# The sync engine's transfers in program order, with the dependent ones placed later

## The chip, the cores and the metric

The kernel runs on one core of a Trainium2 chip. Its time is the device time of one execution in microseconds (us). Five engines work at once: TensorE (PE in the profile; its weight loads are PEld), VectorE (DVE), ScalarE (ACT), GpSimd (POOL) and SyncE (SP). SP computes nothing; it issues all of this kernel's DMA transfers, one after the other, and when the transfer at its head has to wait for data or for a buffer, everything behind it waits too.

## The reference

The input x has 8 sequences of 1024 tokens with 256 values each. The computation is an attention layer and a linear layer, each between a normalization in front and one behind, and each added to its input:

```python
x = x + layernorm(attention(layernorm(x), Wq, Wk, Wv, Wo))
x = x + layernorm(ternary_linear(layernorm(x), weight, alpha, bias))

def attention(x):                       # 16 query heads of 16 values, 4 key/value heads
    q, k, v = x @ Wq, x @ Wk, x @ Wv
    q, k = rope(q), rope(k)             # pairs of values rotated by the token's position
    scores = q k^T / sqrt(256)          # every query with all 1024 keys of its sequence
    return (softmax(scores) @ v) @ Wo

def ternary_linear(x):                  # weights become -1, 0 or 1
    d = 0.7 * mean(|weight|)
    return x @ ((weight > d) - (weight < -d)).T * alpha + bias
```

## The kernel before

**Blocks, groups, windows.** The work is cut into 16 blocks of 512 query tokens (units u = 0 to 15, two for each sequence). A block has four groups; a group i is one query head of each of the four key heads (in the last block, one tile of 128 tokens) against all 1024 keys. The inner loop (`window`, line 1137) runs over s, which counts the exp tiles: 32 a group, 128 a block, 2048 in all. One window takes two or three of them, about 2 us. In a window TensorE multiplies queries and keys for the exp tiles (`exp_one`, line 684; tile se, line 676), ScalarE takes the exponential (line 692, tile e), and TensorE multiplies e of two windows earlier with the values (`av_piece`, line 704, tile av).

**The maxima.** The softmax needs the largest score of each query. The scores are therefore computed twice. Some 40 exp tiles ahead, TensorE computes them in another layout (`max_scores`, line 586; tile sm, line 603) and DVE reduces them (line 628, tile mx). When a group is reduced, its maxima are transposed on TensorE and copied by ScalarE (`shift_rows`, line 649), and DVE makes the second part of them (`shift_low`, line 656, tile ml, line 660). Two DMA transfers on SP then write ml into four rows of the query tile `q_st` (line 667). The exp product of the group multiplies those rows with -1, so the maximum is subtracted inside the product. The first exp product of a group cannot start before its ml has landed.

**Queries and keys.** `q_st` has two buffers, one for each of two successive blocks; `k_st` holds the keys of a sequence and has three. They are made by `Project` two to three blocks ahead. `kv_and_dram` (line 428) multiplies keys and values, stores the keys to DRAM (d_k, line 434) and fetches them back in another layout (k_rot, line 438). `kt` (line 440) rotates and splits them on GpSimd, stores them (dk, line 451) and calls `stack_keys` (line 495), which loads them into `k_st` by six transfers (line 502). `q` rotates and splits the queries on GpSimd and `q_to_dram` (line 487) stores them (dq, line 493). At the start of block u-1 `stack_queries(u)` (line 562) loads them into `q_st`: six transfers of 256 KB (line 567) and two small fills (line 146).

**The tail.** The sums of a group leave through ScalarE (`av_out`, line 720, tile avsb) to DRAM (d_av, line 733). In the block after, `Tail` finishes the layer: it loads x again (xr, line 743), fetches the heads (`fetch`, line 759: two xn and den, lines 763 and 768), inverts the sums on DVE (`invert`, line 772), stores them and loads them back spread out (d_rec line 775, a line 780), scales and splits on GpSimd (`scale`, line 785), multiplies with Wo (`attn`), normalizes, runs the second layer (`xw`, `ffn`), normalizes again (`stats_f`) and stores the output (`end`, line 856).

**The order.** Lists of (step, part) say at which step of four exp tiles each part of a projection (`P_PARTS`) or a tail (`T_PARTS`, and `T_LAST` for the last but one) is issued. At the end of a window `collect` takes the parts that are due into `ready`, and `do_parts` issues them in order; parts that need a PSUM bank (`banked`) come one at a time, in windows of two exp tiles. A part can therefore be issued some windows after its step. For TensorE, DVE and ScalarE this order of issue is the order on the engine: the loop stands in `manual_schedule` for these three. The order on SP and on GpSimd is chosen at build time by a planner that goes by estimated times.

Of the kernel before, what the change touches and what calls it, by code (L numbers as in the profile page):

```python
# [8 lines left out]
F32 = mybir.dt.float32  # L9
# [7 lines left out]
P = 128  # L17
# [11 lines left out]
def kernel(  # L29
# [29 lines left out]
    nc = tc.nc  # L59
    B, S, D = x.shape  # L60
    DK = HKV * HD
# [15 lines left out]
    qkp = ctx.enter_context(tc.tile_pool(name="qkp", bufs=1))  # L77
# [29 lines left out]
    for src, lo, n in ((w_q, 0, D), (w_k, D, DK), (w_v, ROT, DK)):  # L107
        nc.sync.dma_start(
            out=wqkv[:, :, lo : lo + n], in_=src.rearrange("(c p) n -> p c n", p=P)
# [18 lines left out]
    nc.sync.dma_start(out=bias_bc, in_=bias.partition_broadcast(P))  # L128
    alpha_bc = const.tile([P, 1], F32, name="alpha_bc")
    nc.sync.dma_start(out=alpha_bc, in_=alpha.partition_broadcast(P))  # L130


    k_st, v_aug, q_st = [], [], []
# [30 lines left out]
    def split(eng, hi, lo, src, hi_eng=None):  # L164

        split_hi(hi_eng or eng, hi, src)
        split_lo(eng, lo, src, hi)
# [25 lines left out]
    ffn = {}  # L193
# [52 lines left out]
    def ln_apply(eng, dst, src, stats):  # L246
        mv, sc = stats
        for t in range(src.shape[1]):
            if eng is nc.scalar:
                eng.activation(dst[:, t, :], src[:, t, :], AF.Identity, bias=sc[:, 0, t : t + 1])  # L250
                eng.mul(dst[:, t, :], dst[:, t, :], sc[:, 1, t : t + 1])
                continue
            eng.tensor_scalar(  # L253
                dst[:, t, :],
                src[:, t, :],
                sc[:, 0, t : t + 1] if eng is nc.gpsimd else mv[:, t, 0:1],
                sc[:, 1, t : t + 1],
                ALU.add if eng is nc.gpsimd else ALU.subtract,
                ALU.mult,
            )  # L260
# [52 lines left out]
    def rotate(eng, x, cos, sin, t2):  # L313

        for dst, table in ((t2, sin), (x, cos)):
            eng.tensor_tensor(dst, x, table.unsqueeze(1).to_broadcast(list(x.shape)), ALU.mult)  # L316
        eng.tensor_tensor(x[:, 0], x[:, 0], t2[:, 1], ALU.subtract)
        eng.tensor_tensor(x[:, 1], x[:, 1], t2[:, 0], ALU.add)
# [5 lines left out]
    class Project:  # L324
# [103 lines left out]
        def kv_and_dram(self):  # L428

            u = self.u  # L430
            for p in range(2):
                self.kv(p)
            d_k = dram.tile([DK, UQ], F32, tag="d_k", name=f"d_k_{u}")
            nc.sync.dma_start(out=d_k, in_=self.kv_t[:DK])
            self.k_rot = qkp.tile([P, 2, P], F32, tag="k_rot", name=f"k_rot_{u}")
            src = d_k.rearrange("(m e) (g t) -> e g m t", e=2, t=P)
            for e in range(2):
                nc.sync.dma_start(out=self.k_rot[:, e, :], in_=src[e])

        def kt(self):  # L440
            rotate(
                self.eng, self.k_rot, cos_kt_sb[:, self.half], sin_kt_sb[:, self.half],
                work.tile([P, 2, P], F32, tag="t2k", name=f"t2k_{self.u}", bufs=1),
            )
            hl = qkp.tile([P, 2, 2, P], F32R, tag="k_parts", name=f"ks_{self.u}")
            split(self.eng, hl[:, 0], hl[:, 1], self.k_rot)
            dk = self.dk = dram.tile([2, DK, UQ], F32, tag="dk", name=f"dk_{self.u}")
            dst = dk.rearrange("l (m e) (g t) -> l e g m t", e=2, t=P)
            for l in range(2):
                for e in range(2):  # L450
                    nc.sync.dma_start(out=dst[l, e], in_=hl[:, l, e, :].bitcast(F32))
            self.stack_keys()

        def q_product(self, p):
            if self.q_rot is None:
# [31 lines left out]
        def q_to_dram(self):  # L487
            dq[self.u] = dram.tile([2, D, UQ], F32, tag="dq", name=f"dq_{self.u}")
            rows = dq[self.u].rearrange("l (b c i e) t -> l c b i (e t)", c=2, e=2, i=HD // 2)
            for l in range(2):  # L490
                for c in range(2):
                    src = self.hl["q"][64 * c : 64 * (c + 1), l].rearrange("p e t -> p (e t)")
                    nc.sync.dma_start(out=rows[l, c], in_=src.bitcast(F32))
# [242 lines left out]
    class Tail:  # L736
# [21 lines left out]

        def fetch(self):

            for c in range(2):
                self.on[c] = self.new("xn", c)
                nc.sync.dma_start(
                    out=self.on[c].rearrange("p t d -> p (t d)"),
                    in_=d_av[self.u][8 * c : 8 * c + 8, 0:HD, :],
                )
            self.den = small.tile([P, UQ // 8], F32, tag="den", name=f"den_{self.u}", bufs=1)
            nc.sync.dma_start(
                out=self.den, in_=d_av[self.u][:, HD, :].rearrange("i (g t) -> i g t", g=8)
            )  # L770

        def invert(self):
            nc.vector.reciprocal(self.den, self.den)
            d_rec = dram.tile([2, 2 * HKV, UQ], F32, tag="d_rec", name=f"d_rec_{self.u}")
            nc.sync.dma_start(
                out=d_rec.rearrange("c i (g t) -> (c i g) t", g=8), in_=self.den
            )
            for c in range(2):
                self.a[c] = self.new("a", c)
                nc.sync.dma_start(  # L780
                    out=self.a[c].rearrange("p t d -> p (t d)"),
                    in_=d_rec[c].unsqueeze(1).to_broadcast([2 * HKV, HD, UQ]),
                )
# [66 lines left out]
        def end(self, p):  # L850
            u, f = self.u, self.a[p]
            ln_apply(self.eng(p), f, f, self.sc[p])
            self.eng(p).tensor_tensor(f, self.x1[p], f, ALU.add)
            b, half = divmod(u, UPB)
            tiles = out[b, half * UQ : (half + 1) * UQ, :].rearrange("(t p) d -> p t d", p=P)
            nc.sync.dma_start(out=tiles[:, self.tiles(p), :], in_=f)

    class LastTail(Tail):

# [101 lines left out]
    def load(u):  # L961
# [12 lines left out]
        (29, "attn", 2), (29, "x", 1), (30, "stats_a", 2), (30, "ffn", 1), (31, "stats_f", 1),  # L974
    )
    T_PARTS = (
        (1, "fetch"), (7, "invert"), (8, "scale", 0), (9, "scale", 1), (12, "attn", 0),
        (15, "attn", 1), (15, "stats_a", 0), (17, "stats_a", 1), (19, "stats_x", 0),
        (22, "xw", 0), (23, "stats_x", 1), (26, "ffn", 0), (27, "xw", 1), (31, "ffn", 1),
        (31, "stats_f", 0), (33, "stats_f", 1),  # L980
    )

    P_FIRST = (47, 51, 54, 57, 59, 60, 62, 61, 63, 64)
    T_LAST = (1, 3, 4, 5, 9, 10, 11, 14, 17, 19, 20, 22, 25, 27, 24, 28)

    warm = []

# [64 lines left out]
    for u in range(NU - 1):  # L1052
        start = SPU * (u + 1)
        at(start + 1, begin_tail, u)
        steps = [k for k, *_ in T_PARTS] if u < NU - 2 else T_LAST
        for k, (_, *p) in zip(steps, T_PARTS):
# [15 lines left out]
    REGULAR = 40  # L1072
# [5 lines left out]
    def window_size(s):  # L1078


        left = 4 * NK - s % (4 * NK)
        if s >= ends:
            return 4
        if s == 6:
            return 2
        size = min(2 if s >= REGULAR and any(banked(*p) for p in ready) else 3, left, ends - s)
        if left - size == 1:
            size += 1 if size == 2 else -1
        return size
# [23 lines left out]
    def take_low():  # L1113
        while split_later:
            shift_low(split_later.pop(0))
# [12 lines left out]
    def av_windows(lag):  # L1128

        while len(behind) > lag:  # L1130
            i, s, size = behind.pop(0)
            first = s % (4 * NK)
            av_piece(i, first * P, (first + size) * P)
            if first + size == 4 * NK:
                done.append(i)

    def window(s):


        late, size = s >= ends, window_size(s)  # L1140
        if done:
            av_out(done.pop())
        if late:
            for r2 in range(2):
                exp_two(s // 4, r2)
        else:
            end = min(maxima_by(s + size), 4 * NSTEP)
            for q in range(max(size, end - maxima[0])):
                if q < size:
                    exp_one(s + q)  # L1150
                if maxima[0] < end:
                    max_scores(maxima[0])
                    maxima[0] += 1
                if q == 0:
                    take_low()
            reduce_early(maxima[0])
        take_low()
        behind.append((s // (4 * NK), s, size))
        for n in range(s // 4, (s + size) // 4):
            collect(n)  # L1160
        do_parts(3 - size if REGULAR <= s < ends else 99)
        av_windows(1 if late else 2)
        return s + size

    E = mybir.EngineType
    due, picks = [], []
    with tc.manual_schedule(engines={E.PE, E.DVE, E.Activation, E.Pool}):
# [52 lines left out]
        s = 0  # L1220
        while s < 8:
            s = window(s)
    with tc.manual_schedule(engines={E.PE, E.DVE, E.Activation}):
        while s < 4 * NSTEP:
            s = window(s)
        av_windows(0)
        av_out(NU * G - 1)
        assert not (todo or due or ready or split_later)
# [70 lines left out]
```

## Time and profile before

| what | value |
|---|---|
| median of 3 runs | 1698.6 us (1697.74 to 1701.16) |
| the profiled execution, its own time | 1696.64 us |
| its span from the first to the last instruction | 1694.9 us |
| TensorE busy | 1598.8 us, 94% of the span |
| DVE busy | 1398.7 us, 83% |
| ScalarE busy | 1246.4 us, 74% |
| GpSimd busy | 838.5 us, 49% |
| mean granted clock of TensorE | 0.972 |
| DMA moved | 117.95 MB, mean 70 GB/s, nearly all by SP's queue |

The profile is one execution on the chip. In its lines an instruction is named by its line of the kernel and by the tiles it writes and reads (out<-in). A line of a group ends with the busy time, the mean duration of one in ns, the idle time of its engine just before such instructions, and what ended most of it. A wait line reads: who waited, for whom, us in total, how many times, the longest. The chain of waits follows the work that ended last back through what released each step; its lines hold the start, the duration and what it was, and a DMA there runs from its issue to its landing. A timeline line of SP holds the time of issue and how long SP took to issue. The granted clock is the share of full speed that TensorE was given. In a line of a window (from:to) there are the length, the busy time and count of each engine, the granted clock, the share of time that the 16 DMA engines were busy, and GB/s; that share is the sum of the packets' times and can be a little over 1.

### The profile page before, as it was taken

The numbers are of one execution on the slowest core, as the hardware profiler recorded it, in microseconds if no ns is written. First come the engines' busy times: TensorE is split into PE (matmuls) and PEld (weight loads), VectorE is DVE, ScalarE is ACT, GpSimd is POOL, SyncE is SP. The second block draws the span as 40 slices with busy tenths as digits, with TensorE's granted clock in tenths as the row PEclk, the third lists the DMA queues.
The fourth block names the chain that finished last, engine by engine and source line by source line (L and its number), as shares of the span: only waits on it lengthen the run. The fifth ranks groups of instructions, "written<-read, shape, count | busy, mean of one in ns | idle before, by whom it ended". The sixth has DMA issues, their size and how long they took to land.

```text
span 1694.9 us, 36717 instructions
## 1 busy us (share of the span) xinstructions
PE 1598.8 (94%) x14440; PEld 811.3 (48%) x14440; DVE 1398.7 (83%) x2054; ACT 1246.4 (74%) x2423; POOL 838.5 (49%) x1239
## 2 busy tenths in 40 slices
PE   7989899999999999999999999999999999999997
PEld 5544454444545444444444445444444544444444
DVE  7778788979798797978889798797978879998864
ACT  4657677778687786877778687686867768787875
POOL 5541456374554646455464645536455453333444
PEclk8999999999999999999999999999999999999999
DMA  4151514125151432515133151412415124141100
GB/s 134 51 98 37 122 43 95 54 73 98 48 98 57 81 72 65 113 42 100 49 86 80 54 115 45 94 55 71 88 46 100 36 76 74 33 85 33 41 14 26
DMA packets 86077, 117.95 MB, mean 70 GB/s; under 512 B 12088, under 2 KB 50808, under 8 KB 85752
## 3 DMA queue, kind: packets, MB, share of 16 engines
q1 hardware_dynamic: 85904, 115.60, 29.4%
q8 instruction: 114, 1.87, 0.5%
q14 instruction: 59, 0.48, 0.1%
HBM read 68.65 MB, written 45.88 MB: 68 GB/s over the span
## 4 chain that ended last, share of the span: by engine, by line
PE 59%; DVE 22%; DMA 9%; POOL 3%; issue 3%; SPq 2%; ACT 2%; POOLq 0%; ACTq 0%; DVEq 0%
PE av L712 21%; PE se L676 19%; DVE mx L628 18%; PE sm L603 8%; PE pa L302 3%; DMA q_st<-ml 2%; PE pq L302 2%; PE pf L302 2%; DMA dk<-ks 2%; DMA k_rot<-d_k 2%; PE pkv L302 1%; DVE bnst L237 1%; PE pt_ot L279 1%; DMA d_k<-kv_t 1%; ACT e L692 1%
## 5 line engine op out<-in xcount | busy, mean ns | idle before, releaser
L628 DVE TENSOR_REDUCE mx<-sm 128x2 f32<-128x1024 f32 (+1 forms) x1309 | 1205.2, 970 | 244.5 <-PE sm L603 191.3
L692 ACT ACTIVATE e<-se 128x512 f32<-128x512 f32 x1996 | 1053.2, 603 | 301.4 <-PE sm L603 256.6
L603 PE MATMUL sm<-k_st,q_st 64*128 64x512 f32 x2048 | 756.6, 453 | 16.6 <-DVE mx L628 7.7
L676 PE MATMUL se<-q_st,k_st 64*128 64x512 f32 x2048 | 721.7, 448 | 48.4 <-DMA q_st<-ml 42.7
L712 PE MATMUL av<-e,v_aug 128*32 128x256 f32 (+2 forms) x8560 | 612.1, 383 | 0.0
L676 PEld LDWEIGHTS se<-q_st,k_st 64*128 64x128 f32 x2048 | 330.0, 187 | 418.6 <-ACT e L692 240.2
L603 PEld LDWEIGHTS sm<-k_st,q_st 64*128 64x128 f32 x2048 | 329.1, 188 | 94.5 <-DVE mx L628 73.3
L712 PEld LDWEIGHTS av<-e,v_aug 128*32 128x32 f32 x8560 | 196.7, 109 | 233.6 <-issue 171.6
L241 POOL TENSOR_SCALAR lnsc<-mv 128x2 f32<-128x2 f32 (+1 forms) x134 | 25.8, 193 | 287.2 <-DVE mv L239 280.8
L786 POOL TENSOR_TENSOR xn<-xn,a 128x512 f32<-128x512 f32 x30 | 38.5, 1284 | 156.3 <-DMA a<-d_rec 153.9
L242 POOL TENSOR_TENSOR lnsc<-lnsc,mhalf 128x2 f32<-128x2 f32 (+1 forms) x134 | 92.5, 691 | 0.9
L846 POOL TENSOR_TENSOR a<-a,bias_bc 128x512 f32<-128x512 f32 x30 | 38.6, 1285 | 97.9 <-ACT a L845 97.9
L253 POOL TENSOR_SCALAR xn<-x,lnsc 128x256 f32<-128x256 f32 x116 | 65.1, 569 | 2.2
L157 POOL TENSOR_SCALAR ot<-ot 128x512 fp32r<-128x512 f32 x30 | 18.6, 621 | 83.9 <-ACT ot L283 63.7
L316 POOL TENSOR_TENSOR t<-q_rot,sin_q_sb 128x512 f32<-128x512 f32 x31 | 39.8, 1285 | 39.9 <-ACT q_rot L460 39.9
L157 POOL TENSOR_SCALAR xt<-xt 128x512 fp32r<-128x512 f32 x26 | 16.2, 622 | 65.3 <-ACT xt L283 65.3
L302 PE MATMUL pq<-xt,wqkvh 128*128 128x256 f32 x256 | 47.9, 313 | 0.4 <-ACT e L692 0.4
L302 PE MATMUL pa<-woh,hl 128*128 128x256 f32 x240 | 46.2, 294 | 1.1 <-ACT e L692 1.1
L237 DVE BATCH_NORM_STATS2 bnst<-x 128x6 f32<-128x256 f32 x124 | 45.9, 412 | 0.6 <-DMA x<-in_L_attn_x 0.6
L237 DVE BATCH_NORM_STATS2 bnst<-a 128x6 f32<-128x256 f32 x120 | 44.5, 413 | 0.0
L302 PEld LDWEIGHTS pq<-xt,wqkvh 128*128 128x128 f32 x256 | 38.3, 208 | 13.0 <-issue 11.6
L162 POOL TENSOR_TENSOR hlq<-q_rot,hlq 128x512 fp32r<-128x512 f32 x31 | 39.5, 1275 | 7.0 <-ACT hlq L159 4.5
(165 smaller groups left out, 1298.0 us busy)
## 6 DMA issues: line engine op xcount, KB each, us to landing
q_st<-dq SPq DMA_DIRECT2D x90, 256.0 KB
dq<-hlq SPq DMA_DIRECT2D x60, 256.0 KB
d_av<-avsb SPq DMA_DIRECT2D x60, 256.0 KB
x<-in_L_attn_x SPq DMA_DIRECT2D x15, 512.0 KB
xn<-d_av SPq DMA_DIRECT2D x30, 256.0 KB
a<-d_rec SPq DMA_DIRECT2D x30, 256.0 KB
xr<-in_L_attn_x SPq DMA_DIRECT2D x15, 512.0 KB
out_x<-a SPq DMA_DIRECT2D x30, 256.0 KB
```

The costliest lines, as they stand in the source:

```text
L162: eng.tensor_tensor(lo, src, hi.bitcast(F32), ALU.subtract)
L237: nc.vector.bn_stats(st[:, t, :], src[:, t, :])
L242: nc.gpsimd.tensor_tensor(sc[:, 1, :], sc[:, 1, :], mhalf[:, :n], ALU.pow)
L253: eng.tensor_scalar(dst[:, t, :], src[:, t, :], sc[:, 0, t : t + 1] if eng is nc.gpsimd else mv[:, t, 0:1], sc[:, 1, t : t + 1], ALU.add i ...
L302: nc.tensor.matmul(out, chunk(left[i], c), chunk(right[j], c), start=(k == 0), stop=(k == len(steps) - 1),)
L316: eng.tensor_tensor(dst, x, table.unsqueeze(1).to_broadcast(list(x.shape)), ALU.mult)
L603: scores = nc.tensor.matmul(sm[0][:, part, :], queries[rows], k_st[(u // UPB) % 3][rows, r2, ch * 512 : (ch + 1) * 512], start=True, stop= ...
L628: early[0] = nc.vector.tensor_reduce(mx[i][:, a, head_and_tile(i, r2, t), lo:n], sm[0][:, lo:n, :], AX.X, ALU.max).ins
L676: nc.tensor.matmul(sc if len(queries.shape) == 2 else sc.rearrange("p (j t) -> p j t", j=G), k_st[(i // G // UPB) % 3][rows, r2, kt * P : ...
L692: nc.scalar.activation(e, sc, AF.Exp, scale=1.0 / D**0.5)
L712: nc.tensor.matmul(av_ps[0][32 * r : 32 * r + 32, lo:hi], va[:, kt, r, :], es[i * NK + kt, r // 2, r % 2][:, lo:hi], start=(kt == 0 and lo ...
L846: eng.tensor_tensor(f, f, bias, ALU.add)
```

## The change

The main loop, from s = 8 on, gets SP among the engines whose order of issue is fixed, so the planner no longer orders the transfers. So that a transfer does not stand at SP's head long before its data exist, `later(n, f)` puts off its issue by n windows; `queue_postponed` issues what is due in each window, after the exp tiles and maxima of the window and before its parts. Before s = 40 nothing is put off. Put off are the store of d_k (1), the fetch of k_rot (3), the store of dk (4), the load of `k_st` (7), the store of dq (4), the fetch of xn and den (2), the store of d_rec (1), the load of a (3) and the output store (3). Not put off, and so issued where the program has them, are ml, d_av, the loads of x and xr, the load of `q_st` and what the first steps load (the weights of the second layer and Wo). The parts of the tail from `scale` to the second `xw` move one or two steps later in `T_PARTS`, those from `invert` to `attn` and `stats_a` one to four in `T_LAST`.

```diff
+    postponed, window_number, running = [], [0], [False]
+
+    def later(windows, f):
+        if running[0]:
+            postponed.append((window_number[0] + windows, f))
+        else:
+            f()
+
+    def queue_postponed(all_of_them=False):
+        for entry in list(postponed):
+            if all_of_them or entry[0] <= window_number[0]:
+                postponed.remove(entry)
+                entry[1]()
...
-            nc.sync.dma_start(out=d_k, in_=self.kv_t[:DK])
-            self.k_rot = qkp.tile([P, 2, P], F32, tag="k_rot", name=f"k_rot_{u}")
-            src = d_k.rearrange("(m e) (g t) -> e g m t", e=2, t=P)
-            for e in range(2):
-                nc.sync.dma_start(out=self.k_rot[:, e, :], in_=src[e])
+            def fetch():
+                self.k_rot = qkp.tile([P, 2, P], F32, tag="k_rot", name=f"k_rot_{u}")
+                src = d_k.rearrange("(m e) (g t) -> e g m t", e=2, t=P)
+                for e in range(2):
+                    nc.sync.dma_start(out=self.k_rot[:, e, :], in_=src[e])
+
+            later(1, lambda: nc.sync.dma_start(out=d_k, in_=self.kv_t[:DK]))
+            later(3, fetch)
...
-            for l in range(2):
-                for e in range(2):
-                    nc.sync.dma_start(out=dst[l, e], in_=hl[:, l, e, :].bitcast(F32))
-            self.stack_keys()
+            def store():
+                for l in range(2):
+                    for e in range(2):
+                        nc.sync.dma_start(out=dst[l, e], in_=hl[:, l, e, :].bitcast(F32))
+
+            later(4, store)
+            later(7, self.stack_keys)
...
+            later(4, lambda: self.store_q(rows))
+
+        def store_q(self, rows):
...
         def fetch(self):
+            later(2, self.load_heads)
+
+        def load_heads(self):
...
-            nc.sync.dma_start(
+            later(1, lambda: nc.sync.dma_start(
                 out=d_rec.rearrange("c i (g t) -> (c i g) t", g=8), in_=self.den
-            )
+            ))
+            later(3, lambda: self.load_factors(d_rec))
+
+        def load_factors(self, d_rec):
...
-            nc.sync.dma_start(out=tiles[:, self.tiles(p), :], in_=f)
+            later(3, lambda: nc.sync.dma_start(out=tiles[:, self.tiles(p), :], in_=f))
...
-        (1, "fetch"), (7, "invert"), (8, "scale", 0), (9, "scale", 1), (12, "attn", 0),
-        (15, "attn", 1), (15, "stats_a", 0), (17, "stats_a", 1), (19, "stats_x", 0),
-        (22, "xw", 0), (23, "stats_x", 1), (26, "ffn", 0), (27, "xw", 1), (31, "ffn", 1),
+        (1, "fetch"), (7, "invert"), (10, "scale", 0), (11, "scale", 1), (14, "attn", 0),
+        (16, "attn", 1), (16, "stats_a", 0), (18, "stats_a", 1), (20, "stats_x", 0),
+        (23, "xw", 0), (24, "stats_x", 1), (27, "ffn", 0), (28, "xw", 1), (31, "ffn", 1),
         (31, "stats_f", 0), (33, "stats_f", 1),
...
-    T_LAST = (1, 3, 4, 5, 9, 10, 11, 14, 17, 19, 20, 22, 25, 27, 24, 28)
+    T_LAST = (1, 5, 8, 9, 11, 12, 13, 15, 17, 19, 20, 22, 25, 27, 24, 28)
...
+        window_number[0] += 1
+        running[0] = s >= REGULAR
...
         take_low()
+        queue_postponed()
         behind.append((s // (4 * NK), s, size))
...
-    with tc.manual_schedule(engines={E.PE, E.DVE, E.Activation}):
+    with tc.manual_schedule(engines={E.PE, E.DVE, E.Activation, E.SP}):
         while s < 4 * NSTEP:
             s = window(s)
+        running[0] = False
+        queue_postponed(True)
```

## The prediction

> **What bounds the kernel now.** I read the page first, for which engine is full and what it waits for.
>
> ```profile
> PE 1598.8 (94%) x14440; PEld 811.3 (48%) x14440; DVE 1398.7 (83%) x2054; ACT 1246.4 (74%) x2423; POOL 838.5 (49%) x1239
> ...
> L676 PE MATMUL se<-q_st,k_st 64*128 64x512 f32 x2048 | 721.7, 448 | 48.4 <-DMA q_st<-ml 42.7
> ```
>
> TensorE is the bound, and the one thing it waits for in the loop is a DMA: the 8 KB transfer that puts a group's maxima (tile ml) into the query tile. The waits of PE say the same, with the count:
>
> ```profile
> PE se L676 <- DMA q_st<-ml: 42.7, 16, 5.7
> PE sm L603 <- DVE mx L628: 7.7, 25, 1.0
> ```
>
> There are 64 groups and 16 waits. In the timeline of PE they end at 63.04, 91.44, 121.71 (block 0: 2.72, 1.18, 1.59 us), at 204.94 (block 1: 5.71), and then once a block, 257.38 to 1368.47, always before the fourth group of a block: 2.0 to 3.3 us each, 12 of them, 42.7 - 11.2 = 31.5 us. The chain of waits from 625 to 670 us says why that group:
>
> ```profile
> 641.43 2.26 DMA d_k<-kv_t
> ...
> 644.36 3.53 DMA k_rot<-d_k
> ...
> 652.88 3.06 DMA dk<-ks
> ...
> 657.76 1.99 DMA q_st<-ml
> ```
>
> DVE had ml ready at 652.23 (timeline of DVE); SP took it up at 657.76, since it stood in the round trip of the keys (k_rot, GpSimd's rotation, dk, k_st). A free ml lands 1.99 us after its issue.
>
> Each such wait costs more than itself. These windows of 12 us start just before two of them:
>
> ```profile
> 659.00:671.00 12.00, 10.99 (x82) 6.17 (x82) 7.04 (x11) 7.45 (x15) 7.21 (x10) 0.86 0.15 48
> ...
> 860.00:872.00 12.00, 11.19 (x94) 5.74 (x94) 8.70 (x13) 8.41 (x17) 8.69 (x13) 1.00 0.15 46
> ```
>
> Behind the PE, PEld, DVE, ACT and POOL columns, the next number is the granted clock: 0.86 is 1.7 us lost. Over the 12 waits it reads 0.86 five times, 0.72 six times, 1.00 once: 5 x 1.7 + 6 x 3.4 = 28.6 us, 2.4 a wait. The period confirms that nothing gives this back: from wait to wait 659.88 to 760.51 is 100.6, less 2.67 waited and 1.7 of clock 96.3; 860.68 to 960.34 is 99.7, less 3.19 and 0, 96.5. So 60.1 us of the span hang on one late transfer.
>
> Last I read the queue itself at a block's start, as the change reorders it there. SP's timeline (start, length):
>
> ```profile
> 684.48 1.26 SPq L567 DMA_DIRECT2D q_st<-dq  x3
> ...
> 691.84 0.34 SPq L733 DMA_DIRECT2D d_av<-avsb  x1
> 692.95 0.40 SPq L856 DMA_DIRECT2D out_x<-a  x1
> 700.67 0.66 SPq L763 DMA_DIRECT2D xn<-d_av  x1
> ...
> 703.11 1.37 SPq L667 DMA_DIRECT2D q_st<-ml  x2
> ```
>
> and the chain of waits at the start of block 1 (180 to 206 us):
>
> ```profile
> 181.12 4.41 DMA q_st<-dq
> ...
> 185.60 11.78 DMA d_av<-avsb
> ...
> 201.38 3.42 DMA q_st<-ml
> ```
>
> The queries' load (six of 256 KB, two fills) fills the engines: in 686 to 698 the DMA share is 1.08. A store of 256 KB issued behind it took 11.78 us; the same kind at 691.84 made xn wait until 700.67 (7.2 us on SP). What is issued behind this burst lands behind it.
>
> **Part 1: the keys' round trip no longer stands before ml.** By the loop's own order the fourth group's ml is traced three windows behind the fetch of k_rot and three before the store of dk. Nothing then waits in front of it but the load of x, whose buffer was free long before. The lead it has: ready 652.23, needed where PE stopped, 659.88 - 2.74 = 657.14, so 4.9 us against 2.0. The wait goes, and with it the slow clock: -31.5 - 28.6 = -60.1 us.
>
> **Part 2: the queries' load moves behind two stores.** Before, SP issued it at 684.48, when PE had let go of the buffer. In program order it stands behind the store of the block's last sums (d_av, window 3 of the block) and the first output store (three windows behind stats_f of half 0). The first was issued at 691.84, when ACT's copy ended. The second waits for GpSimd's L853, which ended at 692.92; in the changed part lists stats_f of half 0 comes one window later (its s goes from 766 to 768), about 1.8 us on PE, so 692.9 to 694.7. With 0.4 for that issue the burst starts between 693.3 and 695.1; I take 694.4, nearer the later end because the DVE statistics before it move with the window. That is 10 us later than now.
>
> Behind it now come, all ahead of the second group's ml: xr (512 KB), both xn, den, the second output store. Durations: burst and one 256 KB store, 181.12 to 197.38, 16.3 us. xr: an x load took 3.57 in the chain at 12.28, less the 1.99 of a small transfer, 1.6. xn: from 197.38 to 204.8, 7.4 us, five transfers of 256 KB (four dq, one xn), den and ml landed, 1.4 each with 0.4 for the two small ones; two xn are 2.8. So ml lands 16.3 + 1.6 + 2.8 + 0.3 = 21.0 us after the burst's start: 715.4. PE needs it for the 801st exp score, at 709.46 (timeline of PE). New wait: 5.9 us, once a block. Its bounds: 3.7 if the output store is no obstacle (burst at 692.2), 8.5 if GpSimd is 2.5 us later than I take it; below zero is excluded, since even the earliest start of the burst, 692.2, puts its own end at 708.5 with four transfers to come. den lands just before ml, so DVE's reciprocal (709.96) waits some 4.6 us in the same stretch; PE's wait covers it. The clock after it: nearest rows 0 to 3.4, I take the mean 2.4.
>
> Blocks 2 to 12: 11 x (5.9 + 2.4) = +91.3. Blocks 13 and 14 have no wait now but also load queries: ACT's copy ends at 1401.70 and 1493.38, so bursts from 1402.1 and 1494.2, ml at 1423.7 (both output stores behind) and 1515.2, needed at 1418.89 and 1510.56: 4.8 and 4.6, with the clock +14.2. Block 1 waits 5.71 there already; xr, one more xn and six key loads (384 KB, 1.2) join its queue, d_av leaves it, and the burst starts 0.8 later: +4.4. Block 0: weights (256 and 8 x 32 KB) and x of unit 3, which SP had fetched before 62 us, now stand before ml of group 2: 1 MB, +3.2.
>
> **Part 3, at no cost.** The dk, k_st and dq stores and loads move four to seven windows (2 us each) back in the order; k_st and q_st are wanted a block later, which covers them. If that cover went, the maxima would stall. Waits that SP meets there (GpSimd's ks, 5.1 us; hlq, 5.6) have queued behind them: d_av, k_st, dq and, seven or more windows on, the next block's first ml, which has 9.1 us (ready 678.62, needed 687.76), of which latency is 2.0 to 3.9. The scale and attention parts go two or three windows later, with the factors' load; they had 2.3 us (hl done 722.7, first product 725.0) and keep about 4. The last tail's shifts lie in a block without a queries' load.
>
> **Sum.** -60.1 + 91.3 + 14.2 + 4.4 + 3.2 = +53.0 on the profiled execution's 1696.64: 1749.6. The median of the runs is 2.0 above that execution, so 1752.
>
> **The page against the trace.** Two places, which the sum does not need. The row: store d_av, issued behind the burst, 11.78 us. The Trainium skill, DMA: Bandwidth & Descriptors, Queues, rings and completion order, says that an engine takes descriptors in ring order but that completion is not first in, first out for an issuing engine. If ml, which is small, could so land in its free 1.99 us, the new wait would be nil and the sum 1696.6 - 60.1 + 7.6 = 1644; the row says that it does not pass. The other row: 0.86 after a wait of 2.74 us. TensorE: Matmul & The Clock Gate, What's actually happening, lets the clock fall after an idle window of about 3.4 us; by that the 2 to 3 us waits cost no clock, the gain would be 31.5, and only the new wait would lower it: 1778. The trace has the clock fall at 2.0 us, and decides.
>
> **Rivals.** A, the other side: ml does not queue. Something puts it ahead (the burst starts before 688.5, or the small transfer finds its engines free). For: ml's two issues touch four rows of a tile. Against: 11.78 and 3.42 above. It decides once ml lands within 21.7 us of the block's first exp score (709.46 - 687.76); then the time is about 1644. B: the transfers behind the burst overlap its end, so the wait is 1 to 3 us and gain and loss nearly cancel: 11 x (2 + 2.4) + 14 + 7.6 - 60.1 gives 1706. C: SP waits longer for GpSimd, whose order the planner still chooses. A dk or dq store that stands in the way late enough takes 2 us from the first group too: with clock, 12 x 4.4 on top, 1802. D: the order changes little, because the planner's order was the program's: against it, the queries' load now leaves 7 us before the d_av store that precedes it in the program; 1697.
>
> **How the numbers follow.** The forecast 0.70, A 0.14, B 0.06, C 0.08, D 0.02. The forecast's own range is 1725 (wait 3.7) to 1780 (8.5). For 8 in 10 I need B and part of C: 1690 to 1800. 0.2% is about what a measurement of this kernel can tell from no change. Faster: A, a sixth of B and half of D, 0.16; same, the rest of D and a third of B, 0.03; slower, all else, 0.81.
>
> **What would show it.** In the profile after: no PE wait on ml before a fourth group; one before each second group of blocks 2 to 14, 4 to 8 us; SP's L567 issued right behind L733 and L856; the DMA share near 1 until some 22 us into the block; the granted clock below 1 there and not at the keys' round trip; a DVE wait on den about as long. I am wrong if ml of the second group lands within 21.7 us of the block's first exp score, or if SP still issues the queries' load first.

## The result and the profile after

The changed kernel takes 1815.4 us (median of 4 runs, 1809.8 to 1816.8); beside it, on the same chip, the kernel before takes 1698.2 us (4 runs, 1690.0 to 1701.2). The ratio is 1.069, 95% interval 1.065 to 1.074: 117 us slower. The forecast was slower by 53 us, 1752 us in a range of 1690 to 1800. The direction was right, the size was not. The profiled execution of the changed kernel took 1814.7 us, with a span of 1812.9 us.

Most lines of code named here are 16 to 33 higher than before (se is L703, ml L687, its transfers L694, the queries' load L594). The first page of the changed kernel, the engines and two groups:

```profile
PE 1607.7 (89%) x14240; PEld 811.2 (45%) x14240; DVE 1400.1 (77%) x2028; ACT 1249.4 (69%) x2423; POOL 832.4 (46%) x1239
...
L703 PE MATMUL se<-q_st,k_st 64*128 64x512 f32 x2048 | 739.1, 454 | 156.4 <-DMA q_st<-ml 140.2
...
L803 DVE RECIPROCAL den<-den 128x64 f32<-128x64 f32 x15 | 8.3, 552 | 100.7 <-DMA den<-d_av 100.7
```

The computation is nearly as long as before on every engine. What has grown is TensorE's idle time before the exp products, for the same transfer of ml: 140.2 us against 42.7. DVE now waits 100.7 us for den, which lands close to ml; that wait lies in the same stretch as TensorE's. The waits of TensorE count it (us in total, times, longest); the second line, the wait for DVE's maxima, was 7.7 us in 25 waits before:

```profile
PE se L703 <- DMA q_st<-ml: 140.2, 18, 19.0
PE sm L630 <- DVE mx L655: 18.9, 60, 1.0
```

The waits have changed their place. No fourth group waits any more. Instead each second group of blocks 2 to 12 does (6.9 to 9.0 us, mean 8.2), those of blocks 13 and 14 (5.3 and 6.0), that of block 1 (19.0), the third group of block 0 (7.6, where the kernel before had 1.6) and the third group of block 15 (8.4, where it had none).

SP's timeline at the start of block 6, whose first exp product starts at 733.40, shows what stands in front of the second group's ml:

```profile
738.59 0.34 SPq L760 DMA_DIRECT2D d_av<-avsb  x1
741.14 0.41 SPq L889 DMA_DIRECT2D out_x<-a  x1
741.64 2.81 SPq L594 DMA_DIRECT2D q_st<-dq  x6
744.49 0.89 SPq L162 DMA_DIRECT2D q_st<-fill_d  x2
746.18 0.41 SPq L91 DMA_DIRECT2D xr<-in_L_attn_x  x1
748.24 2.66 SPq L793 DMA_DIRECT2D xn<-d_av  x2
752.32 0.55 SPq L798 DMA_DIRECT2D den<-d_av  x1
754.42 0.40 SPq L889 DMA_DIRECT2D out_x<-a  x1
756.47 1.95 SPq L694 DMA_DIRECT2D q_st<-ml  x2
```

The load of the queries starts at 741.64, behind d_av and the first output store. The output store in turn waited for GpSimd, as GpSimd's timeline has it (this addition ends at 741.11):

```profile
739.84 1.27 POOL L886 TENSOR_TENSOR a<-x,a 128x512 f32<-128x512 f32 x1
```

The chain of waits of the same stretch runs through the burst into ml:

```profile
744.02 12.37 DMA q_st<-dq
...
756.47 7.95 DMA q_st<-ml
...
764.56 0.76 PE se L703
```

The values of ml were ready well before that, 18.8 us into the block, as DVE's timeline has it:

```profile
751.83 0.34 DVE L687 SCALAR_TENSOR_TENSOR ml<-mh,low,pm 32x128 fp32r<-32x128 f32 x1
```

With the 1.99 us of a free ml they would have landed before TensorE stopped, so DVE is not what makes ml late. TensorE stopped at 756.10 and went on at 764.56. The landing of each transfer is in the trace; in this block they land in the order of their issue:

| transfer | issued | landed |
|---|---|---|
| q_st, first of six | 741.64 | 746.17 |
| q_st, sixth | 744.02 | 756.39 |
| second fill | 745.15 | 758.84 |
| xr | 746.18 | 760.75 |
| second xn | 750.27 | 763.47 |
| den | 752.32 | 763.65 |
| second output store | 754.42 | 764.24 |
| ml, first of two | 756.47 | 764.42 |

Two things hold ml back. It lands behind some 2.8 MB that were issued ahead of it (six q_st, xr, two xn, a store). And SP cannot even issue it early: xr is issued right behind the landing of the first q_st, ml right behind that of the sixth, each transfer when the one eight places before it has landed. In the trace the transfers use eight semaphores in turn, and these issues wait for the transfer before them on the same semaphore. So this limit is one of the program's waits; no run shows how early ml would land without it.

The waits give a table for the whole kernel. A block runs here from one block's first exp product to the next. "Slow clock" is the time lost to the half clock outside TensorE's longer idle stretches; "short" is all its other idle time.

| blocks | before: length, ml waits, slow clock, short | after | growth |
|---|---|---|---|
| ahead of 0 | 63.0: 2.7, 6.8, 11.3 | 62.7: 2.7, 6.8, 10.9 | -0.3 |
| 0 | 114.4: 2.8, 6.8, 3.9 | 123.2: 8.8, 11.0, 3.7 | +8.8 |
| 1 | 107.8: 8.0, 4.7, 1.6 | 117.3: 19.0, 2.2, 2.6 | +9.5 |
| 2 to 12 | 1112.4: 29.2, 24.6, 19.5 | 1188.4: 90.0, 26.7, 31.7 | +76.0 |
| 13, 14 | 182.0: 0, 0, 4.7 | 198.4: 11.3, 5.6, 4.0 | +16.4 |
| 15 | 115.2: 0, 1.3, 6.7 | 122.9: 8.4, 2.9, 6.4 | +7.7 |

The sum is +118, the difference of the two spans. The ml waits alone are 97.5 of it.

### The profile page after: what moved, and what is told of

Same layout as the page of the kernel before. It is cut to its first block, busy times and chain, and to the rows that moved or that the text cites. A ratio compares the mean times of both kernels' runs of the same rounds, so it can differ in the third digit from the quotient of the medians.

```text
span 1812.9 us, 36134 instructions
## 1 busy us (share of the span) xinstructions
PE 1607.7 (89%) x14240; PEld 811.2 (45%) x14240; DVE 1400.1 (77%) x2028; ACT 1249.4 (69%) x2423; POOL 832.4 (46%) x1239
## 4 chain that ended last, share of the span: by engine, by line
PE 64%; DMA 15%; DVE 12%; POOL 3%; issue 2%; ACT 2%; SPq 1%; POOLq 0%; DVEq 0%; ACTq 0%
PE av L739 23%; PE se L703 22%; DVE mx L655 9%; PE sm L630 7%; DMA q_st<-dq 7%; DMA q_st<-ml 6%; PE pa L318 3%; PE pq L318 2%; PE pf L318 2%; DVE bnst L253 1%; PE pkv L318 1%; ACT e L719 1%; PE pt_ot L295 1%; PE pt_xt L295 1%; DMA xr<-in_L_attn_x 1%
## 5 line engine op out<-in xcount | busy, mean ns | idle before, releaser
L703 PE MATMUL se<-q_st,k_st 64*128 64x512 f32 x2048 | 739.1, 454 | 156.4 <-DMA q_st<-ml 140.2
L630 PE MATMUL sm<-k_st,q_st 64*128 64x512 f32 x2048 | 767.1, 461 | 22.1 <-DVE mx L655 18.9
L703 PEld LDWEIGHTS se<-q_st,k_st 64*128 64x128 f32 x2048 | 339.0, 191 | 539.8 <-ACT e L719 293.6
L630 PEld LDWEIGHTS sm<-k_st,q_st 64*128 64x128 f32 x2048 | 337.5, 192 | 99.8 <-DVE mx L655 77.1
L739 PEld LDWEIGHTS av<-e,v_aug 128*32 128x32 f32 x8360 | 191.3, 110 | 238.8 <-issue 176.4
L803 DVE RECIPROCAL den<-den 128x64 f32<-128x64 f32 x15 | 8.3, 552 | 100.7 <-DMA den<-d_av 100.7
L332 POOL TENSOR_TENSOR t<-q_rot,sin_q_sb 128x512 f32<-128x512 f32 x31 | 39.8, 1283 | 19.8 <-ACT q_rot L484 19.8
L332 POOL TENSOR_TENSOR t2k<-k_rot,sin_kt_sb 128x256 f32<-128x256 f32 x14 | 10.3, 734 | 76.9 <-DMA k_rot<-d_k 76.9
L752 ACT COPY avsb<-av 128x512 f32<-128x512 f32 x63 | 37.9, 602 | 6.0 <-PE av L739 5.8
```

The lines of the kernel that those rows point to most:

```text
L630: scores = nc.tensor.matmul(sm[0][:, part, :], queries[rows], k_st[(u // UPB) % 3][rows, r2, ch * 512 : (ch + 1) * 512], start=True, stop= ...
L703: nc.tensor.matmul(sc if len(queries.shape) == 2 else sc.rearrange("p (j t) -> p j t", j=G), k_st[(i // G // UPB) % 3][rows, r2, kt * P : ...
L739: nc.tensor.matmul(av_ps[0][32 * r : 32 * r + 32, lo:hi], va[:, kt, r, :], es[i * NK + kt, r // 2, r % 2][:, lo:hi], start=(kt == 0 and lo ...
```

## The experiments

Two theories were set against each other. Q: what stands ahead of ml in SP's order, above all the queries' load, makes ml late. S or P: the parts and transfers that the change places later make an engine late, and the wait for the DMA only shows it.

**The queries' load one step earlier**, in the changed kernel:

```diff
-        at(SPU * (u - 1) + 1, stack_queries, u)
+        at(SPU * (u - 1), stack_queries, u)
```

> The changed kernel with one step moved: the queries' load of a block is written one step earlier, so that in SP's order it stands ahead of the store of the block's last sums (d_av) and of the first output store. Theory Q (the second group's wait comes from where the burst of six 256 KB loads stands in SP's queue, since what is issued behind it lands behind it): the burst starts when TensorE lets go of the buffer, some 7 us earlier than in the changed kernel, so the second group's ml lands at about 20.7 us into the block against a need at 22.7. The waits of blocks 2 to 14 vanish or shrink below 1 us, and with them 2.4 us of slow clock each: 13 x 10.2 = 133 us less, about 1683 us; blocks 0, 1 and 15 keep their waits (2.7 + 1.2 + 7.6, 19.0, 8.4 us). Rival S (the parts of the last tail and of the keys that now lie some groups later make DVE, ACT or GpSimd late, and the DMA wait only shows it): the second group's wait stays near 8 us, 1790 to 1816 us.

Measured: 1690.6 us, 0.9968 of the kernel before (0.9954 to 0.9982). One step of the list is worth 125 us, and with it the change is a small gain of 0.3%. SP's timeline at the start of block 6 (first exp product 693.32):

```profile
691.99 2.69 SPq L594 DMA_DIRECT2D q_st<-dq  x6
...
698.50 0.35 SPq L760 DMA_DIRECT2D d_av<-avsb  x1
701.05 0.41 SPq L889 DMA_DIRECT2D out_x<-a  x1
...
712.15 1.39 SPq L694 DMA_DIRECT2D q_st<-ml  x2
```

The same bytes go through the queue, but the load starts 1.3 us before the block's first exp product instead of 8.2 behind it. The second part of ml lands at 715.35, 0.6 us before it is wanted. Theory Q holds, and S falls as the cause of the long waits. The waits for ml are gone in blocks 2 to 14; those that are left are ahead of block 0 and in blocks 0, 1 and 15:

```profile
PE se L703 <- DMA q_st<-ml: 35.9, 5, 18.4
```

It is 8 us above what was expected of it: blocks 2 to 12 take 1084.7 us, of which 33.0 are short waits, against 19.5 before. The last experiment comes back to these.

**The small transfers behind ml**, in the changed kernel, the load left where it is:

```diff
-            self.xr = load_x(u, "xr", 1)
+            if u < NU - 1:
+                later(8, lambda: setattr(self, "xr", load_x(u, "xr", 1)))
+            else:
+                self.xr = load_x(u, "xr", 1)
...
-            later(2, self.load_heads)
+            later(2, self.load_sums)
+            later(8, self.load_heads)
...
+        def load_sums(self):
             self.den = small.tile([P, UQ // 8], F32, tag="den", name=f"den_{self.u}", bufs=1)
...
-            later(3, lambda: nc.sync.dma_start(out=tiles[:, self.tiles(p), :], in_=f))
+            later(8 if p else 3, lambda: nc.sync.dma_start(out=tiles[:, self.tiles(p), :], in_=f))
```

> The changed kernel with the burst left where it is, but four transfers taken out from between it and the second group's ml: the load of the residual x (xr), both loads xn and the second output store are issued some six windows later (8 windows behind their place in the program). Theory Q: ml lands when the burst and den have landed, about 17.7 us behind the burst's start and so 26 us into the block, against a need at 22.7: waits of about 3.3 us instead of 8.2, 13 x 4.9 = 64 us less, about 1752 us, the slow clock as before. Rival S (DMA order isn't the cause): the wait stays near 8 us, about 1815. Rival T (ml waits for the small transfers just ahead of it only, not for the burst): the wait goes, about 1683 us.

Measured: 1738.1 us, 1.026 (1.023 to 1.029). The waits in blocks 2 to 12 are 2.4 to 4.3 us, mean 3.5; those of the whole run:

```profile
PE se L703 <- DMA q_st<-ml: 70.1, 18, 11.5
```

In block 6 the load starts at 709.51 and ml lands at 727.36, 17.9 us behind it instead of 22.8. So the four transfers (xr, two xn, a store) are worth 4.7 us of each wait; the other 3.5 us are left with the load where it stands. Blocks 13 and 14, with waits of 0.9 and 0.6 us, are shorter by 13.9 us and block 1 by 7.5, both more than expected; the time is 14 us below 1752. Rival T (only what is just ahead of ml counts) falls too.

**ml from ScalarE's queue**, in the changed kernel:

```diff
-            shifts[i] = nc.sync.dma_start(out=dst, in_=ml[n * a : n * a + n, :].bitcast(F32)).ins
+            queue = nc.scalar if i >= 3 else nc.sync
+            shifts[i] = queue.dma_start(out=dst, in_=ml[n * a : n * a + n, :].bitcast(F32)).ins
```

> The changed kernel with the two transfers of ml issued from ScalarE's queue instead of SP's, from the fourth group on; all else as it is. Theory Q1 (the wait is SP's order alone: ml can't be issued before what stands ahead of it, and another queue passes it): ml is issued as soon as ScalarE comes to it and lands in some 2 to 4 us, the second groups' waits go, about 1683 us or a little more for what ScalarE's issue costs. Theory Q2 (the burst has filled the engines themselves, whichever queue a transfer comes from): ml is issued at once but lands only with the burst; the wait shrinks by what xr, xn and the store cost (5 us) at most, 1750 us. Rival S: the wait stays, 1815 us.

Measured: 1823.1 us, 1.076 (1.073 to 1.080), no better than the changed kernel. TensorE's waits in this run have a new name, and ScalarE's own say why:

```profile
PE se L704 <- ACT e L720: 117.1, 61, 10.0
...
PE se L704 <- DMA q_st<-ml: 12.5, 3, 8.6
```

```profile
ACT e L720 <- DMA q_st<-fill_d: 69.8, 10, 7.7
```

ScalarE's timeline in one block: an exponential, the two issues of ml, and the next exponential after 7.68 us of idle time.

```profile
749.11 0.60 ACT L720 ACTIVATE e<-se 128x512 f32<-128x512 f32 x1 [0.45 <-PE sm L630]
755.23 2.11 ACTq L695 DMA_DIRECT2D q_st<-ml  x2
757.38 2.07 ACT L720 ACTIVATE e<-se 128x512 f32<-128x512 f32 x4 [7.68 <-DMA q_st<-fill_d]
```

The sixth q_st load landed at 755.14, the first fill at 756.69; ml's two transfers were issued at 755.23 and 756.72. The issue of ml waits here too for the transfer eight places earlier, though SP had issued that one, and now ScalarE with its exponentials stands behind it. Once issued, the first took 6.3 us to land, at 761.52: 22.0 us behind the start of the load, against 22.8 from SP. It passed the second xn, den and the second output store, issued before it from SP (landed at 762.03, 762.41 and 762.86). Whether it would have passed the load this run cannot show, since it was issued only when the load had landed. So none of the three expectations holds as it was put: another queue neither frees ml nor leaves the wait as it was; it hands the wait to ScalarE. The Trainium skill, DMA: Bandwidth & Descriptors, section "Issuing engines are not separate DMA queues", says that transfers started from different engines run on the same 16 DMA engines and that another issuing engine saves only the time to issue; this run agrees as far as it goes: from ScalarE ml took 6.3 us to land, against 1.99 when free, and the median is 8 us above that of the changed kernel.

**The order alone**, in the kernel before:

```diff
-    with tc.manual_schedule(engines={E.PE, E.DVE, E.Activation}):
+    with tc.manual_schedule(engines={E.PE, E.DVE, E.Activation, E.SP}):
```

> The kernel before with the order alone changed: SP's transfers go in the program's order past the second block, with no transfer placed later and the old lists of parts. Theory Q: the queries' load stands behind d_av and the output store as in the changed kernel, so the second group's wait appears here too, 6 to 9 us; beside it SP, in order, waits for GpSimd at dk, dq and d_rec, which the placement was to take away, so further ml transfers are late. 1815 us or more, up to 1950. Rival P (the placement some groups later, not the order, costs the time): no second group's wait, near the kernel before, 1700 us.

Measured: 1861.7 us, 1.098 (1.095 to 1.101). Both waits are there, 5.1 to 8.1 us before the second group of blocks 2 to 14 and 3.2 to 5.9 before the fourth of blocks 1 to 12, and one line counts them all:

```profile
PE se L676 <- DMA q_st<-ml: 173.0, 30, 16.6
```

SP stands at its head for GpSimd as well (the waits of SP in this run):

```profile
SPq L856 <- POOL a L853: 191.8, 25, 12.6
...
SPq L451 <- POOL ks L157: 69.3, 13, 5.6
```

Rival P falls: the order costs the time, and the later placement together with the later lists of parts takes back 46 us of it (1861.7 to 1815.4).

**The placement alone**, in the changed kernel:

```diff
-    with tc.manual_schedule(engines={E.PE, E.DVE, E.Activation, E.SP}):
+    with tc.manual_schedule(engines={E.PE, E.DVE, E.Activation}):
```

> The changed kernel with SP's order left to the planner: the transfers placed some groups later and the later parts of the last tail stay, only SP is taken out of the engines that keep the program's order. Theory Q (the order put the queries' load behind d_av and the first output store): SP issues the load again when TensorE lets go of the buffer, so no second group waits; what the placement does to the fourth group is open: 1640 us if its wait goes too, 1700 us if it stays. Rival P (the later placement costs the time): a second group's wait of 8 us and 1790 to 1815 us.

Measured: 1680.9 us, 0.991 (0.989 to 0.994), between the two cases named. With the planner the load starts 1.3 us before the first exp product of blocks 2 to 12, and no second group of blocks 2 to 14 waits; that of block 1 still does, for 6.9 us. The fourth group's waits are 0.3 to 1.5 us, once 2.9, instead of 2 to 3.3. All waits for ml in this run:

```profile
PE se L703 <- DMA q_st<-ml: 25.5, 16, 6.9
```

So the half of the change that the prediction put at no cost is a gain of 0.9% by itself.

**The first output store behind the load**, in the changed kernel. It tests one term of the prediction, the start of the load:

```diff
-            later(3, lambda: nc.sync.dma_start(out=tiles[:, self.tiles(p), :], in_=f))
+            later(3 if p else 5, lambda: nc.sync.dma_start(out=tiles[:, self.tiles(p), :], in_=f))
```

> The changed kernel with the first output store two windows later, behind the queries' load instead of ahead of it, the load itself in its place. It tests why the burst started at 8.2 us into the block and not at 6.6: SP waits at that store for GpSimd. Theory Q: the burst then starts behind d_av alone, some 2.4 us earlier, and the store's transfer still lands ahead of ml: waits of 5.8 instead of 8.2 us in blocks 2 to 14, 13 x 2.4 = 31 us less, 1784 us. Rival (the start of the burst is set by something else, or the burst has its own time whenever it starts): 1810 to 1820 us.

Measured: 1788.8 us, 1.054 (1.052 to 1.056). SP's timeline in block 6 (first exp product 721.48) has the load at 5.6 us into the block:

```profile
726.67 0.34 SPq L760 DMA_DIRECT2D d_av<-avsb  x1
727.12 2.78 SPq L594 DMA_DIRECT2D q_st<-dq  x6
```

The mean wait in blocks 2 to 12 falls from 8.2 to 5.9 us, by 2.3, as the load comes 2.6 us earlier in its block. In these blocks SP's wait for GpSimd at one store, in front of the load, goes straight into TensorE's wait. Blocks 13 and 14 gain nothing (waits of 7.4 and 5.4 us, against 5.3 and 6.0), and the time is 5 us above the 1784 expected.

**The order mended in blocks 0, 1 and 15**, on top of the first experiment:

```diff
-            self.xr = load_x(u, "xr", 1)
+            self.xr = load_x(u, "x", 2) if u == NU - 1 else load_x(u, "xr", 1)
...
-            later(7, self.stack_keys)
+            later(14 if self.u == 3 else 7, self.stack_keys)
...
-            later(4, lambda: self.store_q(rows))
+            later(12 if self.u == 3 else 4, lambda: self.store_q(rows))
...
-                (7, measure), (9, prepare_wo), (11, add_up), (13, threshold), (15, ternarize),
+                (7, measure), (11, add_up), (13, threshold), (15, ternarize), (16, prepare_wo),
...
-        at(SPU * (u - 1) + 1, stack_queries, u)
+        at(SPU * (u - 1) - (u == 2), stack_queries, u)
```

Its reason lies in the changed kernel's trace. In block 1, in the chain, the load of the queries starts at 194.85, 8.9 us into the block (before: 181.12, 3.7 us into it), since SP stood at the store dk (the first line, from SP's timeline) until GpSimd had the keys of unit 3; and xr, k_st, dq, xn and den are all issued before ml, which lands 31.7 us behind the start of the load (before: 23.7):

```profile
189.95 4.25 SPq L473 DMA_DIRECT2D dk<-ks  x4
```

```profile
194.85 5.26 DMA q_st<-dq
...
200.12 13.67 DMA xr<-in_L_attn_x
...
222.67 3.93 DMA q_st<-ml
```

In block 15 the load of xr has one buffer, which the tail before still reads. The waits of SP and its timeline (ml was ready at 1729.47):

```profile
SPq L91 <- POOL x L851: 30.1, 1, 30.1
```

```profile
1741.86 0.37 SPq L91 DMA_DIRECT2D xr<-in_L_attn_x  x1
1742.34 1.38 SPq L694 DMA_DIRECT2D q_st<-ml  x2
```

> The first of these kernels (queries' load one step earlier) with the three waits mended that it still shows. Block 15: the last x (xr of unit 15) goes into a buffer of tile x, which is free, so that its load does not stand at SP's head for 30 us in front of ml. Block 0: the eight loads of wo come from step 16 instead of 9, behind ml of the third group. Block 1: the queries' load is written before the block's first step, so ahead of the store dk of unit 3, and k_st and dq of unit 3 come behind ml of the second group. Theory Q (each of these waits is what stands ahead of ml in SP's queue): block 15 -8.6 -2.8, block 0 -5.0, block 1 -18.4 with perhaps 1 to 5 us back for the clock: 1690.6 - 34.8 + 3 = 1659 us, 0.979 of the kernel before. Rival: ml is made late there by DVE (the maxima of block 15, the key chain of block 1), and the wait only turns into one on DVE: 1680 to 1690 us.

Measured: 1657.8 us, 0.977 (0.975 to 0.979); expected were 1659. Against the first experiment block 15 went from 123.1 to 113.3 us, block 1 from 117.6 to 97.7 and block 0 from 117.9 to 116.6, where 3.1 us of wait are left. Three waits for ml remain in the whole run, all ahead of or in block 0; the short waits of TensorE for DVE's maxima and for ScalarE are now the longer items:

```profile
PE sm L630 <- DVE mx L655: 19.1, 61, 1.0
PE se L703 <- ACT e L719: 13.5, 30, 0.5
PE se L703 <- DMA q_st<-ml: 7.0, 3, 3.1
```

**The old list for the later half of the tail**, on top of that. The list changed is `T_PARTS`, which the tails of units 0 to 13 use; the text below calls it the last tail's:

```diff
-        (16, "attn", 1), (16, "stats_a", 0), (18, "stats_a", 1), (20, "stats_x", 0),
-        (23, "xw", 0), (24, "stats_x", 1), (27, "ffn", 0), (28, "xw", 1), (31, "ffn", 1),
+        (15, "attn", 1), (15, "stats_a", 0), (17, "stats_a", 1), (19, "stats_x", 0),
+        (22, "xw", 0), (23, "stats_x", 1), (26, "ffn", 0), (27, "xw", 1), (31, "ffn", 1),
```

> The mended kernel (e6_order_mended) with the second half of the last tail's list put back to where the kernel before has it: the second attn product and the parts behind it one step earlier; scale and the first attn product stay where the change put them. In the traces of placement alone and of the mended kernel TensorE loses about 1 us a block more in short waits (0.4 to 0.6 us each, at steps 6, 20, 22 and 26 of a block, for DVE's maxima and ACT's exponentials) than before. Theory L (these come from the later list, whose statistics now fall beside the maxima that a group starts from): most of it goes, 11 to 13 blocks x 0.8 us, about 10 us less, 1648 us. Rival O (they come from SP's order or from the faster run itself): 1655 to 1661 us, and the short waits stay. A cost is possible too: if GpSimd is not done with the second half when its product comes, TensorE waits 1 to 2 us a block, 1670 us or more.

Measured: 1639.6 us, 0.967 (0.965 to 0.969), the best kernel of this study, 3.3% faster than the kernel before. The short waits fall to nearly what they were before (7.7 and 3.2 us):

```profile
PE sm L630 <- DVE mx L655: 7.8, 25, 1.0
...
PE se L703 <- ACT e L719: 3.5, 8, 0.5
```

Blocks 2 to 12 take 1063.4 us instead of 1081.7. Of these 18.3 us, 11.1 are short waits and the other 7.2 lie inside TensorE's busy time. Theory L holds for the waits; the gain was nearly twice what it promised. What the 7.2 are is open: the later list also cuts the loop's windows differently (14,240 matmuls in the changed kernel, 14,432 here, 14,440 in the kernel before), and no run separates the cut of the windows from the place of the statistics.

## Why the prediction was right in kind and wrong in size

The prediction's sum was +53.0, the traces' is +118. Three of its steps failed. In Part 2 the start of the queries' load and the time from there to ml's landing were put too low (25 us of the miss, in blocks 2 to 12), and so was what stands ahead of ml in blocks 0 and 1 (16 us). In Part 3 the later places of parts and transfers were put at no cost and cost 20 us. Step by step, with the table above:

**Part 1, the fourth group's wait goes: right.** None of the 12 waits is left, and that includes the half clock behind them. Its -60.1 us shows undisturbed only in the last experiment: blocks 2 to 12 take 1063.4 us there against 1112.4 before, -49.0; the forecast's share of these 11 blocks is 11/12 of 60.1, 55.1. The waits and the slow clock that are gone there come to 53.8; 4.8 us of other short waits and busy time take part of it back. In the changed kernel itself the waits of the second groups hide it.

**Part 2, the load behind d_av and the output store: the mechanism right, three terms mis-sized.** The wait was to be 5.9 us and is 8.2 in blocks 2 to 12, so 11 x 2.3 = 25 us more. In block 6 the load starts 8.2 us into the block, not 6.6, since the output store ahead of it waits for GpSimd's addition, which ends 7.7 us into the block: later than the whole range that the prediction gave the start, 5.5 to 7.3. The upper bound of 8.5 us of wait was nearly reached. ml lands 22.8 us behind the start of the load, not 21.0: by the table of landings the load with its fills and the store took 17.8 us, not 16.3, and xr 1.9, not 1.6. The need is at 22.7 us, not 21.7. That makes +1.6 + 1.8 - 1.0 = 2.4. With the store taken away from before the load, so that it starts at 5.6, the wait measured 5.9, with the two other errors still in it. The slow clock behind the wait, 2.4 us, was right: 26.7 us over 11 blocks. Where the prediction set a row against a page, the rows were the better guide. In block 6 SP's small ml landed behind all that was issued ahead of it (7.9 us to its landing, against 1.99 when free), though not everywhere: in block 1 it landed at 226.60 and den, issued 0.9 us before it, at 227.08. And the slow clock of blocks 2 to 12, 24.6 us before, is 0 in the last two kernels, where the waits of 2 to 3 us are gone.

**Blocks 13 and 14**: +14.2 forecast, +16.4 measured.

**Block 1**: the forecast's +4.4, less the wait of its fourth group that Part 1 takes (a twelfth of 60.1, 5.0), is -0.6; measured +9.5. What failed is "the burst starts 0.8 later". Against its block it started 5.2 us later, because the store dk stood at SP's head for GpSimd, and ml then needed 8.0 us more behind it. This is rival C, in one place: the list of what would join the queue was right, the wait of SP was not seen, and the price of the list was too low.

**Block 0**: +3.2 forecast, +8.8 measured. The forecast priced the bytes of wo and x ahead of ml and took the rest as hidden. SP issued wo only as earlier transfers landed: 115.25 to 125.15, while ml was ready at 114.69.

**Part 3, "at no cost"**: two misses. "The last tail's shifts lie in a block without a queries' load" looked at one load only; the load of xr that stood at SP's head for GpSimd made block 15 7.7 us longer. And the later list for the tail's parts cost TensorE 12 us of short waits in blocks 2 to 12 (19.5 to 31.7); putting its second half back, in the mended order, gained 18. The kernel with the order alone, which has the old list, has 18.0 us of short waits there, so the order does not make them.

**The sum of the misses**: blocks 2 to 12 +76.0 measured against +91.3 - 55.1 = +36.2, that is 39.8 (25 wait, 12 short waits, the rest the clock and busy time); block 1 10.1; block 0 5.6; blocks 13 and 14 2.2; block 15 7.7; less 0.3: 65.

**The rivals.** A (ml does not queue) did not occur. Even in the first experiment ml lands 23.4 us behind the start of the load in block 6; the wait is gone because the load starts earlier. The prediction's point for A, a landing within 21.7 us of the block's first exp product, was a little too strict: there ml lands at 22.0 and is wanted at 22.6. A's 1644 us was reached (1639.6) only with blocks 0, 1 and 15 and the tail's list put right as well. B and D did not occur: the wait was 8.2 us, not 1 to 3, and the planner's order is far from the program's, since leaving the order to the planner makes the changed kernel 135 us faster.

## What to carry to other kernels

A fixed order on the queue of transfers is only as good as the position of its largest burst. Here what was issued behind the burst landed behind it, so a large load belongs at the first moment its buffer is free, and a store that waits for a slow engine does not belong in front of it. Look for every transfer that can wait at the head of an in-order queue, by block and also in the first and last blocks: here each such wait (2.6 us for an output store, 30 for one load at the end) went on, in whole or in part, to the transfer that TensorE needed. Price a moved list of parts too, even where the work is the same: one step cost a microsecond and more a block.

## What was not expected of the hardware

Another issuing engine did not give the urgent transfer a free way: it too was issued only when the transfer eight places before it had landed, it landed 22.0 us behind the start of the burst from ScalarE and 22.8 from SP, and the engine that issued it stood still for 7.7 us.

The granted clock fell after shorter waits than the 2.0 us that the prediction had seen, and not after each. In the kernel before, the clock stayed at 1.00 after a wait of 2.18 us, and in the second experiment after one of 2.88 us (block 11). In the first experiment, TensorE's timeline and a window (busy times, clock, DMA share, GB/s, as before):

```profile
669.03 0.98 PE L295 MATMUL pt_ot<-ident,xn 128*128 128x128 f32 x4 [1.71 <-POOL xn L269]
```

```profile
670.00:676.00 6.00, 5.89 (x42) 2.39 (x41) 4.43 (x9) 4.85 (x10) 5.92 (x7) 0.72 0.21 66
```

With the placement alone:

```profile
555.99 0.46 PE L703 MATMUL se<-q_st,k_st 64*128 64x512 f32 x1 [1.53 <-DMA q_st<-ml]
```

```profile
555.00:561.00 6.00, 5.01 (x44) 2.37 (x44) 3.61 (x5) 4.22 (x9) 5.92 (x7) 1.00 0.50 144
```

After 1.71 us of idle time the clock was 0.72 of full for 6 us, that is 1.7 us lost; after 1.53 us it stayed at 1.00. The half clock lasts 3.413 us or a multiple of it in nearly every case of these traces. A wait of 8 us cost no more of it (2.4 us a block) than one of 2.7 did before (24.6 us over 11 blocks, 2.2). The Trainium skill, TensorE: Matmul & The Clock Gate, section "What's actually happening", gives an idle window of about 3.4 us as what lowers the clock; the length of the half-clock stretches agrees with that figure, the length of the waits that set them off does not.
